# Outer product p7's additions in another order and on GpSimd, the last bias added by pieces, squares summed over both heads of a pair

## The chip, the cores and the metric

The kernel runs on one core of one Trainium2 chip. Its metric is the device time of one execution in microseconds (us). The engines of the core are named as the profile names them: PE is TensorE's matmul side and PEld its weight loads, DVE is VectorE, ACT is ScalarE, POOL is GpSimd, and SP is SyncE, which here only issues DMAs. Each engine runs its own instructions in order, and they wait for each other through semaphores. All numbers are float32.

## The reference

There are 2048 tokens (8 x 256) of 512 values and two layers. The part that the change touches is the first layer's attention, with 32 heads of 128:

```python
qkv = jax.nn.silu(hidden_states @ qkv_w.T)          # 32 heads x (q, k, v) x 128
...
attn = ...                                          # scores with decay, no softmax
xf = xf * jax.lax.rsqrt(jnp.mean(xf * xf, axis=-1, keepdims=True) + EPS)
normed = norm_w * xf.astype(attn.dtype)
gate = jax.nn.sigmoid(hidden_states @ gate_w.T)
return gate * normed @ out_w.T
...
x = x + _L0_attn_ref(xn, ...) + _L0_ffn_ref(xn, ...)
```

The mean of squares runs over all 32 heads (4096 values a token). Beside the attention stands a mixture of 16 experts, two a token, and a shared expert; `sb3` is the bias of the shared expert's last product, 512 values added to every token. A second layer with a small attention and a low-rank mixture follows.

## The kernel before, in words

The tokens are worked in four chunks i = 0 to 3 of 512 (two batches of 256), and the heads in eight groups g of four. A pair (i, g) is a unit. In a unit the projection of a chunk to q, k, gate and v of four heads is done by Strassen's scheme in Winograd's form, on two levels. The outer level has seven products, in the order `p1, p2, p6, p5, p3, p7, p4` (class `Outer`); each of them is itself split in the same way into seven inner products (methods `p1` to `p7` of `Outer`), each written by eight hardware matmuls into a PSUM bank of 128x512. Chunk 0 does four of its seven outer products plainly (`plain`), with eight products, while it builds sums of weights that later chunks load. There are three kinds of banks here: `ps_a` (two), `ps_b` and `ps_e` (one each). For an outer product n the main loop (lines 1318 to 1363) issues its inner p1 and p7, then p3 of outer product n - 1, then p6, p4, p2, p5.

`result` (L1106) reads out each of the four finished quarters (i, j) of an outer product, in the order (1, 0), (0, 0), (1, 1), (0, 1). It puts them together with four accumulators of 128x4x512: `a`, `b`, `c`, `d`. Outer p1 makes `a`, p2 makes `b`, p5 makes `c`, p3 makes `d`; p6, p7 and p4 are first read out from the bank to a temporary `r` (three buffers, tag `sum`, shared with the experts' results `ye` of L820) and then added: p6 and p4 to `a`, p7 to `a` and to `c`. Reading out is a VectorE addition of the bank and an earlier copy (L1134), for the last quarter a ScalarE copy (L1132). The addition to `a` runs on GpSimd (L1135), that to `c`, for p7, on VectorE (L1138). Copies of banks that an inner product goes on accumulating in are made by ScalarE (`copied`, L1101).

When an accumulator is whole, a `Quarter` of attention begins (L1139 to L1141): `b` after p2, `d` after p3, `c` after p7, `a` after p4, for one pair of heads and one batch each. Its pieces (SiLU, gate, scores, attend) are not issued at once. `later(after, f)` (L751) puts a piece into a list with a due slot, and `slot()` (L755), called once after every inner product, issues those that are due: one a slot, two while more than twelve wait; the pieces that its list names (those with little or no work for PE) don't count. There are 49 slots in a unit. The experts' steps, the chunk's ending and the building of tables go the same way. ACT and POOL run their instructions in the order in which the program issues them (L660); on the other engines and for the DMAs the scheduler may move them, except those that are marked to keep their order.

`attend` (L864) squares the 128x512 result of a pair of heads (L884) and adds it on GpSimd to `sums`, 512 values for each batch (L885); the first pair of a chunk is squared into `sums` directly (L881), and after the last pair the two heads' halves are added (L887). `output` (L914) makes sums and differences of gated results `gT` for the output projection, which is Strassen's too; its weights `wo` lie in a ring of seven buffers (L1001). In chunk 1 four differences of these weights are made on GpSimd in every unit (`out_sum`, L1005). The output projection adds up in `acc`, which there is once.

At the end of a chunk, `load_sum` (L1023) reloads the sum `r` of input and shared expert and calls `last_bias` (L651), which loads the bias `sb3` into a buffer of the ring `sum` and issues its four additions to GpSimd at once. After the last projection, `done` (L1030) issues the mean of squares, on POOL the combination of `acc`'s seven parts, on DVE `finish` (L640), which adds the scaled attention to `r`, and a store.

`read_table` (L1204) loads the list of tokens of each expert in two halves, each into the buffer `sq` of the squares; `take_table` copies it out 40 slots later (L1224).

Of the kernel before, what the change touches and what calls it, by code (L numbers as in the profile page):

```python
# [9 lines left out]
FP = mybir.dt.float32  # L10
# [8 lines left out]
B, S, C = 8, 256, 512  # L19
# [51 lines left out]
def block_kernel(  # L71
# [588 lines left out]
    with tc.tile_pool(name="attn", bufs=1) as attn, tc.manual_schedule(engines={mybir.EngineType.Activation, mybir.EngineType.Pool}):  # L660
# [94 lines left out]
        def slot():  # L755

            now[0] += 1
            n = 0
            while pieces and pieces[0][0] <= now[0] and n < (2 if len(pieces) > 12 else 1):
                f = pieces.pop(0)[2]  # L760
                f()
                n += getattr(f, "func", f).__name__ not in ("silu", "bias", "gate", "read_table", "take_table", "scatter", "load_sum", "sums1", "sums2", "sums3", "sums4", "settle0", "settle1", "out_sum", "combine", "finish", "store")


        class Expert:
# [48 lines left out]
            def down(self):  # L814
                py = ps_y()
                mm(  # L816
                    py, self.he, self.we[:, 2 * NC * INTER : 2 * NC * INTER + C],
                    start=True, stop=True,
                )
                ye = attn.tile([P, C], FP, tag="sum", name="ye", bufs=3)  # L820
                add(ye, py, self.xe)
                nc.sync.dma_start(out=yd[bass.ts(self.j, P), :], in_=ye)


        class Quarter:
# [15 lines left out]
            def begin(self):  # L841
                if self.u.g == NG - 1 and (self.pair, self.b) == (1, 0):
                    later(5, self.u.load_sum)
                later(2, partial(self.silu, 0))
                later(3, partial(self.silu, 1))
                later(4, self.gate)
                later(7, partial(self.scores, 0))
                later(8, partial(self.scores, 1))
                later(12, partial(self.attend, 0))
                later(13, partial(self.attend, 1))  # L850
# [13 lines left out]
            def attend(self, hh):  # L864
# [12 lines left out]
                if u.i not in sums_:  # L877
                    sums_[u.i] = attn.tile([P, 2, CH], FP, tag="sums", name="sums")
                sums = sums_[u.i][:, self.b, :]
                if u.g == 0 and self.pair == 0:  # L880
                    nc.scalar.activation(sums, po, AF.Square)  # L881
                else:
                    sq = attn.tile([P, CH], FP, tag="sq" if u.i else "cp", name="sq", bufs=1 if u.i else 5)
                    nc.scalar.activation(sq, po, AF.Square)  # L884
                    add(sums, sums, sq, nc.gpsimd)  # L885
                if u.g == NG - 1 and self.pair == 1:
                    add(sums[:, 0:S], sums[:, 0:S], sums[:, S:], nc.gpsimd)  # L887
                gT = u.gated()
# [11 lines left out]
        class Unit:  # L900
# [122 lines left out]
            def load_sum(self):  # L1023

                if self.i + 1 < NCH:
                    self.r = spare8()
                    nc.sync.dma_start(out=self.r, in_=xr[self.i])
                    last_bias(self.r, attn.tile([P, C], FP, tag="sum", name="sb3", bufs=3))

# [34 lines left out]
        class Outer:  # L1064


            def __init__(self, unit, p):
                self.u, self.p = unit, p
                self.steps = []
                self.following = None  # L1070
# [35 lines left out]
            def result(self, i, j, bank, c):  # L1106
# [22 lines left out]
                else:  # L1129
                    r = attn.tile([P, 512], FP, tag="sum", name="r", bufs=3)  # L1130
                    if c is None:
                        nc.scalar.copy(r, bank)  # L1132
                    else:
                        add(r, bank, c)  # L1134
                    add(a, a, r, pool)  # L1135
                    if p == "p7":
                        c_ = u.tile("c")[:, q]
                        add(c_, c_, r)  # L1138
                whole = dict(p2=("b", 0, 0), p3=("d", 0, 1), p7=("c", 1, 1), p4=("a", 1, 0)).get(p)  # L1139
# [64 lines left out]
        def read_table(n=0):  # L1204
# [18 lines left out]

            later(40, take_table)  # L1224

# [571 lines left out]
```

## Time and profile before

| | |
|---|---|
| time of three runs | 2783.33, 2780.84, 2780.56 us; median 2780.84 |
| the profiled execution | 2780.53 us, of it 2778.5 from the first to the last instruction |
| granted TensorE clock, mean | 0.997 |
| chunk 0 to 3 of the attention | about 130 to 2465 us |
| additions `c<-c,r` on VectorE | 96, 1557 ns mean, 146.7 us |
| additions `c<-c,r` on GpSimd (`a`, from p6, p7, p4) | 264, 1332 ns mean, 345.8 us |
| reading out `r` on VectorE | 240, 684 to 686 ns |

In the profile all of the accumulators are named `c`, and every addition has the line of the helper that records it, L100, so they are told apart by engine and operands. A row of the waits says who waited for whom, how long in total, how often, and at most. A row of the order in time has start, length, engine, line, operation, operands, count, and in brackets how long the engine was idle before it and what ended that. Matmul ends are modelled, and idle times under 0.15 us are taken for the pipeline's own.

### The profile page before, as it was taken

To read this page: it belongs to the slowest core of one execution; us is meant where nothing else is said; L and a number is where in the kernel's file an instruction comes from. 1 tells how busy PE (TensorE), PEld (TensorE's weight loads), DVE (VectorE), ACT (ScalarE), POOL (GpSimd) and SP (SyncE) were. 2 spreads that over 40 slices of the span, in tenths; PEclk is the share of its full clock that TensorE was granted. 3 is DMA by queue.
4 is the path that set the end of the run, shared out by engine and by line. 5 is a ranking of instruction groups with operands and counts; after the bars stand their busy time and mean duration, and the time that the engine had idled before them with its cause. 6 is when DMAs were issued, how large, how long until landed. Compare 5 with 4: busy or idle time off the path is not lost.

```text
span 2778.5 us, 49222 instructions
## 1 busy us (share of the span) xinstructions
PE 2733.5 (98%) x19492; PEld 2522.7 (91%) x19492; DVE 1627.6 (59%) x2733; ACT 947.2 (34%) x1683; POOL 1649.8 (59%) x1422
## 2 busy tenths in 40 slices
PE   9999999999999999999999999999999999999999
PEld 5699999999999999999999999999999999987877
DVE  7656777776545555555545555555555555667663
ACT  5232222222433333333343333334433333432221
POOL 6477777776566666665855555556555567553210
PEclk9999999999999999999999999999999999999999
DMA  7898898888977777777877777787877788653211
GB/s 296 310 339 335 311 334 325 337 315 330 352 274 261 288 272 277 265 280 288 304 250 253 253 257 251 264 288 268 281 255 255 270 298 295 218 215 124 78 63 63
DMA packets 155445, 735.87 MB, mean 265 GB/s; under 512 B 18768, under 2 KB 25296, under 8 KB 112848
## 3 DMA queue, kind: packets, MB, share of 16 engines
q1 hardware_dynamic: 137056, 661.89, 64.8%
q0 software_dynamic: 17872, 70.32, 7.7%
q8 instruction: 154, 2.52, 0.4%
q14 instruction: 75, 0.61, 0.1%
q10 hardware_dynamic: 288, 0.52, 0.1%
HBM read 587.84 MB, written 144.04 MB: 263 GB/s over the span
## 4 chain that ended last, share of the span: by engine, by line
PE 86%; DVE 6%; POOL 3%; issue 3%; DMA 2%; ACT 0%; SPq 0%; DVEq 0%; POOLq 0%; ACTq 0%
PE ps_a L735 25%; PE ps_e L735 13%; PE ps_sc L948 10%; PE ps_b L735 7%; PE ps_sc L968 4%; PE ps_o L869 4%; PE ps_sc L857 3%; PE ps_sc L804 3%; PE ps_o L870 2%; PE ps_sc L858 2%; PE ps_a L1676 2%; PE ps_sc L816 1%; DVE w L100 1%; PE ps_a L1579 1%; PE ps_a L359 1%
## 5 line engine op out<-in xcount | busy, mean ns | idle before, releaser
L735 PE MATMUL ps_a<-xt,w 128*128 128x128 f32 x5376 | 751.3, 276 | 16.3 <-DVE r L100 7.6
L735 PEld LDWEIGHTS ps_a<-xt,w 128*128 128x128 f32 x5376 | 686.7, 192 | 46.0 <-issue 14.1
L100 POOL TENSOR_TENSOR c<-c 128x512 f32<-128x512 f32 x240 | 305.2, 1286 | 265.7 <-DVE c L100 263.1
L1103 ACT COPY cp<-ps_a 128x512 f32<-128x512 f32 x384 | 224.0, 584 | 659.9 <-PE ps_a L735 636.9
L100 POOL TENSOR_TENSOR c<-c,r 128x512 f32<-128x512 f32 x264 | 345.8, 1332 | 167.1 <-DVE r L100 166.6
L735 PE MATMUL ps_e<-xt,w 128*128 128x128 f32 x2688 | 374.5, 275 | 0.6 <-DVE r L100 0.3
L735 PEld LDWEIGHTS ps_e<-xt,w 128*128 128x128 f32 x2688 | 341.4, 192 | 6.7 <-issue 2.9
L735 PE MATMUL ps_a<-w,xt 128*128 128x128 f32 x1792 | 346.8, 275 | 0.0
L100 POOL TENSOR_TENSOR w<-w 128x512 f32<-128x512 f32 x224 | 297.7, 1337 | 80.5 <-DVE w L100 32.9
L100 POOL TENSOR_TENSOR sums<-sums,sq 128x512 f32<-128x512 f32 x120 | 155.8, 1298 | 277.4 <-ACT sq L884 276.8
L948 PE MATMUL ps_sc<-wo,gT 128*128 128x256 f32 x1288 | 304.9, 380 | 2.8 <-POOL gT L100 2.8
L735 PEld LDWEIGHTS ps_a<-w,xt 128*128 128x128 f32 x1792 | 272.4, 192 | 0.0
L948 PEld LDWEIGHTS ps_sc<-wo,gT 128*128 128x128 f32 x1288 | 232.9, 190 | 30.9 <-POOL gT L100 3.1
L100 DVE TENSOR_TENSOR acc<-ps_sc,acc 128x512 f32<-128x512 f32 x208 | 142.7, 689 | 195.2 <-PE ps_sc L948 150.6
L891 DVE SCALAR_TENSOR_TENSOR gT<-ps_o,nw,c 128x256 f32<-128x256 f32 x256 | 112.0, 479 | 216.1 <-ACT sq L884 206.0
L735 PE MATMUL ps_b<-xt,w 128*128 128x128 f32 x1536 | 214.8, 276 | 6.5 <-issue 3.7
L100 DVE TENSOR_TENSOR c<-ps_a,c 128x512 f32<-128x512 f32 x216 | 146.8, 687 | 120.7 <-PE ps_a L735 115.4
L735 PEld LDWEIGHTS ps_b<-xt,w 128*128 128x128 f32 x1536 | 195.1, 193 | 9.0 <-issue 5.7
L832 ACT ACTIVATE c<-c 128x512 f32<-128x512 f32 x256 | 150.3, 628 | 146.0 <-DVE c L100 127.9
L884 ACT ACTIVATE sq<-ps_o 128x512 f32<-128x512 f32 x120 | 71.7, 597 | 358.1 <-PE ps_o L870 352.7
L100 DVE TENSOR_TENSOR s<-ps_sc,decay 128x384 f32<-128x384 f32 x256 | 139.7, 553 | 79.9 <-PE ps_sc L858 77.2
L735 PE MATMUL ps_e<-w,xt 128*128 128x128 f32 x896 | 173.5, 275 | 0.0
(297 smaller groups left out, 4723.3 us busy)
## 6 DMA issues: line engine op xcount, KB each, us to landing
w<-in_w_att_dram SPq DMA_DIRECT2D x56, 1024.0 KB
w<-in_w_att_dram SPq DMA_DIRECT2D x72, 768.0 KB
st<-in_w_att_dram SPq DMA_DIRECT2D x32, 1024.0 KB
wo<-in_w_out_dram SPq DMA_DIRECT2D x113, 256.0 KB
decay<-dec SPq DMA_DIRECT2D x64, 384.0 KB
w<-ws0p SPq DMA_DIRECT2D x12, 1792.0 KB
w<-ws1p SPq DMA_DIRECT2D x12, 1792.0 KB
w<-ws2p SPq DMA_DIRECT2D x12, 1792.0 KB
```

Of the source, the lines that this page charges most:

```text
L100: (eng or nc.vector).tensor_tensor(o, a, b, op)
L735: mm(bank[:, bass.ts(ty, P)], a, b, start=(first and ty == 0), stop=True, skip_group_check=True,)
L804: mm(pu[:, bass.ts(n, P)], w12[:, n, c, :], self.xeT[:, c, :], start=(c == 0), stop=(c == NC - 1),)
L832: nc.scalar.activation(qk, qk, AF.Silu)
L857: mm(p[:, 0:S], self.c[:, 2 * hh, P : 2 * P], q, start=True, stop=True)
L858: mm(p[:, S : S + P], self.c[:, 2 * hh + 1, P : 2 * P], q[:, 1, :], start=True, stop=True,)
L869: mm(po[:, bass.ts(hh, S)], v[:, 0, :], self.s[:, hh, 0:S], start=True, stop=False)
L884: nc.scalar.activation(sq, po, AF.Square)
L891: nc.vector.scalar_tensor_tensor(gT[:, h, :].rearrange("p (t n) -> p t n", t=2), po[:, bass.ts(h, S)].rearrange("p (t n) -> p t n", t=2), ...
L948: mm(py[:, bass.ts(t, S)], self.O[p][:, hh, bass.ts(t, P)], self.wo[p][:, hh, :], start=(t == 0 and hh == 0), stop=(hh == 1), skip_group_c ...
L968: mm(py[:, bass.ts(h, S)], gT[:, hh, bass.ts(t, P)], self.wo[pair, h][:, hh, :], start=(h == 0 and hh == 0), stop=(hh == 1), skip_group_ch ...
L1103: nc.scalar.copy(c, bank)
```

## The change

- In `result`, for p7 outside chunk 0, the additions to `c` go to GpSimd at each readout, and those to `a` to VectorE. The latter are collected and issued after the third readout (three of them), and after the fourth.
- `r` and `ye` have four buffers. The room comes from `sums`, which holds 256 values for each batch instead of 512: each square goes to a buffer of its own, and its two heads' halves are added to `sums` by two instructions (one for the first pair).
- `load_sum` is issued after one slot instead of five. The bias goes to a buffer of the ring `wo`, and its four additions become pieces 10, 13, 16 and 19 slots later, which don't count in a slot.
- `take_table` comes after 30 slots.

```diff
@@ slot
-                n += getattr(f, "func", f).__name__ not in ("silu", "bias", "gate", ...
+                n += getattr(f, "func", f).__name__ not in ("bias_sum", "silu", "bias", "gate", ...
@@ Expert.down
-                ye = attn.tile([P, C], FP, tag="sum", name="ye", bufs=3)
+                ye = attn.tile([P, C], FP, tag="sum", name="ye", bufs=4)
@@ Quarter.begin
-                    later(5, self.u.load_sum)
+                    later(1, self.u.load_sum)
@@ Quarter.attend
-                    sums_[u.i] = attn.tile([P, 2, CH], FP, tag="sums", name="sums")
+                    sums_[u.i] = attn.tile([P, 2, S], FP, tag="sums", name="sums")
                 sums = sums_[u.i][:, self.b, :]
+                sq = attn.tile([P, CH], FP, tag="sq" if u.i else "cp", name="sq", bufs=1 if u.i else 5)
+                nc.scalar.activation(sq, po, AF.Square)
                 if u.g == 0 and self.pair == 0:
-                    nc.scalar.activation(sums, po, AF.Square)
+                    add(sums, sq[:, 0:S], sq[:, S:], nc.gpsimd)
                 else:
-                    sq = attn.tile([P, CH], FP, tag="sq" if u.i else "cp", name="sq", bufs=1 if u.i else 5)
-                    nc.scalar.activation(sq, po, AF.Square)
-                    add(sums, sums, sq, nc.gpsimd)
-                if u.g == NG - 1 and self.pair == 1:
-                    add(sums[:, 0:S], sums[:, 0:S], sums[:, S:], nc.gpsimd)
+                    for h in range(2):
+                        add(sums, sums, sq[:, bass.ts(h, S)], nc.gpsimd)
@@ Unit.load_sum
-                    last_bias(self.r, attn.tile([P, C], FP, tag="sum", name="sb3", bufs=3))
+                    b3_t = attn.tile([P, C], FP, tag="wo", name="sb3", bufs=7)
+                    nc.sync.dma_start(out=b3_t, in_=b3[E : E + 1].to_broadcast([P, C]))
+
+                    def bias_sum(t):
+                        add(self.r[:, t, :], self.r[:, t, :], b3_t, nc.gpsimd)
+
+                    for t in range(TPC):
+                        later(10 + 3 * t, partial(bias_sum, t))
@@ Outer
-                self.steps = []
+                self.steps, self.added = [], []
...
-                    r = attn.tile([P, 512], FP, tag="sum", name="r", bufs=3)
+                    r = attn.tile([P, 512], FP, tag="sum", name="r", bufs=4)
                     if c is None:
                         nc.scalar.copy(r, bank)
                     else:
                         add(r, bank, c)
-                    add(a, a, r, pool)
-                    if p == "p7":
+                    if p != "p7":
+                        add(a, a, r, pool)
+                    else:
                         c_ = u.tile("c")[:, q]
-                        add(c_, c_, r)
+                        add(c_, c_, r, pool)
+
+                        self.added.append(partial(add, a, a, r))
+                        if (i, j) in ((1, 1), (0, 1)):
+                            while self.added:
+                                self.added.pop(0)()
@@ read_table
-            later(40, take_table)
+            later(30, take_table)
```

More of the change, by code (lines that the diff above doesn't have):

```diff
@@ L761, in slot @@
                 f()
-                n += getattr(f, "func", f).__name__ not in ("silu", "bias", "gate", "read_table", "take_table", "scatter", "load_sum", "sums1", "sums2", "sums3", "sums4", "settle0", "settle1", "out_sum", "combine", "finish", "store")
+                n += getattr(f, "func", f).__name__ not in ("bias_sum", "silu", "bias", "gate", "read_table", "take_table", "scatter", "load_sum", "sums1", "sums2", "sums3", "sums4", "settle0", "settle1", "out_sum", "combine", "finish", "store")
         class Expert:
```

## The prediction

> **What bounds the kernel now.** I read the page's first part, then the chain of waits, then TensorE's own list of waits, and last the instructions in order of time around each wait.
>
> ```profile
> PE 2733.5 (98%) x19492; PEld 2522.7 (91%) x19492; DVE 1627.6 (59%) x2733; ACT 947.2 (34%) x1683; POOL 1649.8 (59%) x1422
> PE 86%; DVE 6%; POOL 3%; issue 3%; DMA 2%; ACT 0%; SPq 0%; DVEq 0%; POOLq 0%; ACTq 0%
> ```
>
> TensorE is busy for 2733.5 of 2778.5 us and holds 86% of the chain. The change touches no matmul, so it can win only out of the 45 us in which TensorE idles, and it loses only where it makes TensorE wait. The list of TensorE's waits (us in total, times, longest) names the part within reach:
>
> ```profile
> PE ps_a L735 <- DVE r L100: 7.6, 16, 1.3
> PE ps_a L735 <- ACT cp L1103: 5.2, 3, 1.8
> ...
> PE ps_sc L948 <- POOL gT L100: 2.8, 2, 1.6
> ```
>
> Asked by stretches, the sixteen waits for `r` all lie in chunks i = 1 to 3: thirteen of 0.4 us, two of 0.5, one of 1.3. Chunk 0 has none. Here is one of the thirteen, in order of time (start, length, instruction; idle before it in brackets):
>
> ```profile
> 1445.35 0.69 DVE L100 TENSOR_TENSOR r<-ps_e,cp 128x512 f32<-128x512 f32 x1 [1.19 <-PE ps_e L735]
> 1446.12 1.27 POOL L100 TENSOR_TENSOR c<-c,r 128x512 f32<-128x512 f32 x1 [4.09 <-DVE r L100]
> 1446.14 1.80 DVE L100 TENSOR_TENSOR c<-c,r 128x512 f32<-128x512 f32 x1
> 1446.84 0.83 PE L735 MATMUL ps_a<-xt,w 128*128 128x128 f32 x6
> 1447.73 0.83 PE L735 MATMUL ps_e<-xt,w 128*128 128x128 f32 x6
> 1447.87 0.68 DVE L100 TENSOR_TENSOR r<-ps_b,cp 128x512 f32<-128x512 f32 x1
> 1448.47 0.68 DVE L100 TENSOR_TENSOR r<-ps_a,cp 128x512 f32<-128x512 f32 x1
> 1448.62 4.62 POOL L100 TENSOR_TENSOR c<-c,r 128x512 f32<-128x512 f32 x3 [1.23 <-DVE r L100]
> 1449.06 4.73 DVE L100 TENSOR_TENSOR c<-c,r 128x512 f32<-128x512 f32 x3
> 1449.20 0.94 PE L735 MATMUL ps_a<-xt,w 128*128 128x128 f32 x6 [0.41 <-DVE r L100]
> ```
>
> Products start 0.89 us apart (1446.84, 1447.73), so the next was due at 1448.63. It came at 1449.20, 0.57 late, because it accumulates into the bank that the third `r` reads out. That readout stood behind an addition of 1.80 us on VectorE.
>
> **The change, part by part.**
>
> *Outer product p7 (96 additions to `c` leave VectorE for GpSimd, 96 to `a` go the other way).* Counts stay, order changes: the readouts come first, and VectorE's additions follow in a burst after the third. In the stretch above the second readout can begin about 0.13 us after its bank is done, near 1446.25, and the third near 1447.15, ending 1447.85. The product is due at 1448.63: slack 0.8, the whole 0.57 is won. Thirteen such places: **-7.4 us**.
>
> What is late next? Single additions on VectorE take 0.68 us with GpSimd still, 1.75 to 1.80 beside a GpSimd addition, and GpSimd's own take 1.27, or 1.73 when one of VectorE's gets between. The Trainium skill ("SBUF — State Buffer", section "SBUF: two separate sides") has a rule that speaks against the swap: a VectorE operation with two SBUF inputs and a GpSimd operation that reads SBUF exclude each other for the whole instruction, so moving additions between the two frees nothing. By the rule, eight additions hold the port for 4 x 0.68 + 4 x 1.27 = 7.8 us either way; the trace has 1446.12 to 1453.80, 7.7 us, and agrees. I take no gain of engine time, and the gain above is order alone. It differs on one price: under the rule a VectorE addition caught by GpSimd lasts 1.27 + 0.68 = 1.95, the row says 1.80 at most, and four at the rule's price would end 0.6 us later. I take the row.
>
> So VectorE's fourth addition ends near 1453.8 as before, while TensorE is 0.57 ahead. The following Outer's third readout ended at 1456.53 for a product at 1457.52: slack 0.99 becomes 0.42. Nothing is given back.
>
> `c` feeds the next quarter of attention, and its last addition is now GpSimd's fourth instead of VectorE's. In the trace GpSimd's fourth (to `a`) already ends 0.58 us or more before that SiLU starts in fifteen of the sixteen units of chunks 2 and 3 (the last unit I leave out), so ScalarE starts no later there. In chunk 1, GpSimd's queue holds the four output-weight differences and an expert's bias gather between the third and fourth addition:
>
> ```profile
> 1149.72 1.29 POOL L100 TENSOR_TENSOR wo<-wo 128x512 f32<-128x512 f32 x1
> 1150.12 1.14 ACT L832 ACTIVATE c<-c 128x512 f32<-128x512 f32 x2
> 1150.95 2.51 POOL L100 TENSOR_TENSOR c<-c,r 128x512 f32<-128x512 f32 x2
> 1156.30 0.83 PE L735 MATMUL ps_a<-xt,w 128*128 128x128 f32 x6
> ```
>
> There the fourth ends at 1152.23, 2.1 us after the SiLU starts. The SiLU waits; queued behind it on ScalarE are two SiLUs, gate and tanh, then the bank copy that started 2.84 us after it. That copy would end at 1152.27 + 2.84 + 0.56 = 1155.67, and its product starts at 1156.30: slack 0.63, cost 0 in seven units. In unit (1,0) the delay is 3.7 us and eats part of what is won there.
>
> *Four buffers for `r` instead of three.* Two waits of 0.65 us (1380.8 and 1969.2, units (2,0) and (3,0)) and the one of 1.49 (772.1) are readouts that wait for a buffer held by GpSimd's backlog. A fourth buffer removes both of the first, -1.2, and about 0.9 of the third, after 0.5 given back to the late SiLU: **-2.1 us**. Experts' results share this ring; three `r` held for the burst leave one.
>
> *Last bias.* Now GpSimd stands before four additions until a transfer lands:
>
> ```profile
> 1309.78 0.33 SPq L653 DMA_DIRECT2D sb<-in_b_dram  x1
> 1322.60 4.96 POOL L100 TENSOR_TENSOR spare<-spare,sb 128x512 f32<-128x512 f32 x4 [11.43 <-DMA sb<-in_b_dram]
> ```
>
> It waits 11.4 us, adds for 5.0, and the gated differences behind it hold TensorE for 1.8 us at 1328.9 (the list's 1.6 and its ramp). The other two places (721 and 1901) hold up nothing on TensorE. Afterwards the two DMAs issue four slots earlier on SyncE, the additions come one by one from ten slots on, some 15 us after the issue (a unit of 49 slots takes 73 to 76 us) against 12.7 us to landing. **-1.8 us.** The bias takes a buffer of the output weights' ring; each following weight load then reuses the next tile along, released two slots or more before: nothing. The slots of all other pieces stay within two of their place; the `finish` steps keep theirs, so the two 1.8 us waits for ScalarE's copies (1364, 1952), which stand behind `finish`, stay.
>
> *Squares.*
>
> ```profile
> L100 POOL TENSOR_TENSOR sums<-sums,sq 128x512 f32<-128x512 f32 x120 | 155.8, 1298 | 277.4 <-ACT sq L884 276.8
> L100 POOL TENSOR_TENSOR sums<-sums 128x256 f32<-128x256 f32 x8 | 5.8, 726 | 0.6
> ```
>
> 120 additions of 1.298 become 240 of 0.726, eight of 0.726 move from the end to the beginning: GpSimd +18.4 us, 0.15 each quarter, at 59% load. ScalarE's 128 squares stay. Cover: GpSimd's idle time. It is thin in chunk 0, where TensorE waits five times, 3.2 us, for weight sums on GpSimd: five delays of 0.15 would be 0.8, none falling there 0. I take +0.5. The wait for `gT` at 2334 grows by 0.15.
>
> *Table read ten slots earlier.* It frees the `sq` buffer for chunk 1's first square, which now uses it. Its VectorE copy runs 30 slots, some 45 us, after the read's issue: nothing.
>
> Sum: -7.4 - 2.1 - 1.8 + 0.65 = -10.7 us. Each removed wait lets later work arrive sooner, and waits under 0.15 us are not listed; I keep nine tenths, -9.5. Against the profiled execution (2778.5 us span, 2780.53 in all) that is 2771.0; the median shown, 2780.84, is 0.3 us above it. **Forecast 2771 us**, 0.35% faster. Own range: 2768 (all 12.5 won without cost) to 2775 (half).
>
> **Rivals.**
>
> *The wait returns one Outer later.* The slack of 0.42 in front of the following Outer's product is used up, as VectorE's burst ends half a microsecond late. For it: additions of 1.8 us exist. Against: the port's sum is unchanged. Then the thirteen win nothing, and 2.1 + 1.8 - 0.65 remain: about 2777, no change that can be measured (0.2%, 5.6 us, is what this kernel's times tell from none).
>
> *The burst holds VectorE: slower.* If all four additions run at 1.8, they end at 1447.85 + 7.2 = 1455.05, 1.25 later than now. In thirteen units of chunks 2 and 3 the next readout is then 1.25 - 0.42 = 0.83 late against 0.57 won: +3.4. In chunk 1 the burst stands in front of the expert's transposed rows (a copy that ends at 1147.72 for a product at 1147.86): 1.1 late in seven units, +7.7. With -3.3 elsewhere: +7.8, about 2788. It decides from a mean of 1.6 us for these additions (now 1.557). Against it: a burst begun while GpSimd works catches the same gaps between its additions as today.
>
> *The new order isn't what the engines run.* VectorE's order is not held by hand except for marked steps; if the additions to `a` are put between the readouts again, only buffers and bias pay: 2777, as the first rival.
>
> **Chances.** Forecast 0.66; the wait returns or the order is not kept, 0.18; slower 0.16. Single ends shift a little: faster by over 0.2% 0.66, within 0.17, slower 0.17. A range of 2767 to 2782 holds the forecast's cases and nearly all of the middle.
>
> **What would show it.** TensorE's list loses the sixteen waits for `r`, and the one for `gT` near 1329; the additions to `a` on VectorE stand three in a row after the third readout; GpSimd's `spare` additions stand singly with no idle time for `sb`; GpSimd is 18 us busier. It is wrong if waits for ScalarE's `cp` appear in chunk 1 (late SiLU), for `xeT` (burst), or for weights in chunk 0.

## The result, and the profile after

The changed kernel takes 2775.07 us (median of 20 runs, 2770.12 to 2782.01), the kernel before beside it on the same chip 2782.01 us (20 runs). The ratio is **0.9975, 95% interval 0.9968 to 0.9982**: 0.25% faster, or some 7.0 us (5.0 to 8.9) of 2780.84. The forecast was 0.35%, 9.5 us. The profiled execution took 2772.59 us with a span of 2770.6, against 2780.53 and 2778.5.

The first part of the page (busy us, share of the span, instructions):

```profile
PE 2730.1 (99%) x19492; PEld 2523.7 (91%) x19492; DVE 1614.9 (58%) x2733; ACT 949.2 (34%) x1683; POOL 1682.5 (61%) x1542
```

TensorE's instructions are as many as before, and GpSimd has 120 more and is 33 us busier: 25 from the squares (187.0 for 161.6; forecast 18, at 0.726 us each; they took 0.75) and 14 from slower additions to the accumulators, less what other groups lost. TensorE's list of waits (us in total, times, longest):

```profile
PE ps_a L735 <- ACT cp L1109: 6.5, 3, 2.3
PE ps_a L735 <- POOL w L100: 3.9, 5, 1.4
...
PE ps_e L735 <- DVE r L100: 2.1, 3, 1.0
...
PE ps_sc L947 <- POOL gT L100: 1.4, 1, 1.4
```

The row of sixteen waits of `ps_a` for `r`, 7.6 us, is gone, and so is one of the two for `gT`. Four rows of the attention have grown: ScalarE's copies from 5.2 to 6.5, weight sums from 3.2 to 3.9, `ps_e` waiting for `r` from 0.3 to 2.1, and `ps_o` waiting for `s` (chunk 0) from 1.3 to 1.8.

The list counts from the modelled end of the matmul before, which lies 0.16 us behind the start that its successor has without a wait; so each wait is 0.16 us longer than listed (0.57 where the row in the prediction has 0.41; the prediction calls this a ramp). So I also took, for each matmul, the time from its start to the next one's, less the median for its kind, and added up what exceeds 0.12 us:

| TensorE's lost time, us | before | after |
|---|---|---|
| before chunk 0, to 130 us | 9.7 | 9.6 |
| chunk 0, 130 to 755 us | 15.5 | 16.5 |
| chunks 1 to 3, 755 to 2470 us | 17.6 | 10.4 |
| after 2470 us | 10.3 | 9.7 |

In chunks 1 to 3 the thirteen waits of 0.57 are gone (7.4), that of 1.49 at 772 and that of 1.81 at 1329. Against them stand +1.3 at two chunk endings (1.83 and 1.84 became 2.50 and 2.48), +1.0 in units (2,0) and (3,0) (0.65 twice became 1.18 and 1.10), and 1.4 in four small places.

The table still leaves out that the next matmul after a late one follows it by 0.21 us instead of 0.11. The time from one unit's first readout of p7 to the next unit's has this in it: from unit (2,1) on it was 73.18 us before (1445.35 to 1518.53) and is 72.50 now (1444.87 to 1517.37). In nine units nothing else changed, and they are 0.67 to 0.70 us shorter. So my estimate for the thirteen waits is 13 x 0.68 = 8.8 us; the new waits have the same addition, and the sum for chunks 1 to 3 stays near the 7.2 of the table.

Here is the place that the prediction showed, unit (2,1), in the changed kernel, in order of time:

```profile
1444.87 0.69 DVE L100 TENSOR_TENSOR r<-ps_e,cp 128x512 f32<-128x512 f32 x1 [1.19 <-PE ps_e L735]
1445.66 0.69 DVE L100 TENSOR_TENSOR c<-c,r 128x512 f32<-128x512 f32 x1
1445.70 6.38 POOL L100 TENSOR_TENSOR c<-c,r 128x512 f32<-128x512 f32 x4 [4.22 <-DVE r L100]
1446.27 0.69 DVE L100 TENSOR_TENSOR r<-ps_b,cp 128x512 f32<-128x512 f32 x1
1446.87 0.68 DVE L100 TENSOR_TENSOR r<-ps_a,cp 128x512 f32<-128x512 f32 x1
...
1447.47 5.16 DVE L100 TENSOR_TENSOR c<-c,r 128x512 f32<-128x512 f32 x3
...
1448.14 0.83 PE L735 MATMUL ps_a<-xt,w 128*128 128x128 f32 x6
```

The product at 1448.14 has no wait. But **the order on VectorE is not the forecast one**: readout, addition, readout, readout, three additions is the kernel before's own order. The additions were collected in the program, and the scheduler, which may move VectorE's unmarked instructions, put the first behind the first readout again. What differs is its length: 0.69 us where it was 1.80. And it now begins at 1445.66, 0.04 ahead of GpSimd's at 1445.70; before, GpSimd's began at 1446.12 and VectorE's at 1446.14.

Measured from the end of the first readout, this is so in every one of twenty p7 of chunks 1 to 3 (the other four of the 24 have another order or other starts there):

| | GpSimd's addition begins | VectorE's addition begins | VectorE's takes | GpSimd's takes |
|---|---|---|---|---|
| before | 79 ns | 104 ns | 1.80 us | 1.27 us |
| after | 143 to 144 ns | 104 ns | 0.69 us | 1.79 us |

Thirteen of the twenty, those of chunks 2 and 3, had the waits of 0.57. The seven of chunk 1 had the same 1.80 before and lost 0.14 at most: there an expert's four matmuls (L786, 0.44 us) stand ahead of the product that needs the bank.

The groups say the same over all additions (busy us, mean ns):

```profile
L100 POOL TENSOR_TENSOR c<-c,r 128x512 f32<-128x512 f32 x264 | 359.4, 1384 | 154.1 <-DVE r L100 153.5
...
L100 DVE TENSOR_TENSOR c<-c,r 128x512 f32<-128x512 f32 x96 | 135.3, 1438 | 2.1
```

VectorE's fell from 1557 to 1438 ns, GpSimd's rose from 1332 to 1384. In all the additions take 494.7 us against 492.5: nothing was saved, only the one that waits changed.

### The profile page after: what moved, and what is told of

It is laid out like the page before. It is cut to its first block, busy times and chain, and to the rows that moved or that the text cites. A ratio compares the mean times of both kernels' runs of the same rounds, so it can differ in the third digit from the quotient of the medians.

```text
span 2770.6 us, 49302 instructions
## 1 busy us (share of the span) xinstructions
PE 2730.1 (99%) x19492; PEld 2523.7 (91%) x19492; DVE 1614.9 (58%) x2733; ACT 949.2 (34%) x1683; POOL 1682.5 (61%) x1542
## 5 line engine op out<-in xcount | busy, mean ns | idle before, releaser
L735 PE MATMUL ps_a<-xt,w 128*128 128x128 f32 x5376 | 751.0, 276 | 10.7 <-ACT cp L1109 6.5
L100 POOL TENSOR_TENSOR c<-c,r 128x512 f32<-128x512 f32 x264 | 359.4, 1384 | 154.1 <-DVE r L100 153.5
L100 POOL TENSOR_TENSOR sums<-sums,sq 128x256 f32<-128x256 f32 x240 | 180.2, 751 | 287.1 <-ACT sq L881 277.3
L100 DVE TENSOR_TENSOR acc<-ps_sc,acc 128x512 f32<-128x512 f32 x208 | 142.7, 689 | 203.3 <-PE ps_sc L947 161.6
```

The lines of the kernel that those rows point to most:

```text
L100: (eng or nc.vector).tensor_tensor(o, a, b, op)
L735: mm(bank[:, bass.ts(ty, P)], a, b, start=(first and ty == 0), stop=True, skip_group_check=True,)
```

## The experiments

**Theory 1:** the 7.4 us come from who begins first after the first readout (before, GpSimd by 25 ns; after, VectorE by 40). The one that comes second waits for the other. If that is VectorE, the second and third readouts stand behind it and TensorE waits; if it is GpSimd, nobody does. **Theory 2** (the prediction's): they come from taking the additions from between the readouts. **Theory 3:** they come from which engine adds to which accumulator, whoever begins first. The recorded expectations count their theories anew for each run: their "theory 2" is theory 2 here for the first four kernels, theory 3 for dve_later2 and dve_later3, and the prediction's slower rival for forced.

### Who begins first: six kernels

*at_once*: the changed kernel, additions to `a` issued at each readout.

```diff
-                        self.added.append(partial(add, a, a, r))
-                        if (i, j) in ((1, 1), (0, 1)):
-                            while self.added:
-                                self.added.pop(0)()
+                        add(a, a, r)
```

> The changed kernel, but VectorE's additions to a are issued at each readout, not collected behind the third. Theory 1 (the thirteen 0.57 us waits vanished because VectorE's first addition is first at the port, 0.69 us instead of 1.80; collecting changed nothing in VectorE's order): no wait of TensorE for r on ps_a in chunks 2 and 3, the first addition of a group at about 0.69, span within 2 us of 2770.6. Theory 2 (collecting keeps the readouts free): the thirteen waits of 0.4 us return, span about 2778.

*collect_only*: the changed kernel, `a` on GpSimd and `c` on VectorE as before, still collected.

```diff
-                        add(c_, c_, r, pool)
+                        add(a, a, r, pool)
...
-                        self.added.append(partial(add, a, a, r))
+                        self.added.append(partial(add, c_, c_, r))
```

> The changed kernel, but a stays with GpSimd and c with VectorE as before; VectorE's additions (to c) are still collected. Theory 1: GpSimd's addition to a waits for one engine only, starts before VectorE's, the first addition of a group takes 1.80 and the thirteen waits of 0.4 us stay (0.57 each, 7.4 us): span 2776 to 2779. Theory 2 (order alone): the waits are gone, span about 2771.

*pool_later*: the kernel before, and one tiny copy on GpSimd.

```diff
+                    if p == "p7" and (i, j) == (1, 0):
+                        pool.tensor_copy(small.tile([P, 1], FP, tag="tiny", name="tiny"), r[:, 0:1])
                     add(a, a, r, pool)
```

> The kernel before with one instruction more in each p7: GpSimd copies one column of the first r to a spare tile ahead of its first addition to a, so that this addition starts some 0.1 us later. Nothing else is changed. Theory 1: VectorE's first addition is first at the port and takes about 0.7 us; the thirteen waits vanish, span 2770 to 2772 with everything else as before. Theory 2: nothing changes, span 2778 to 2779.

*dve_later*: the changed kernel, and one tiny copy on VectorE. The condition around it is the same as in pool_later.

```diff
+                        if (i, j) == (1, 0):
+                            tiny = small.tile([P, 1], FP, tag="tiny", name="tiny")
+                            self.added.append(partial(nc.vector.tensor_copy, tiny, r[:, 0:1]))
                         self.added.append(partial(add, a, a, r))
```

> The changed kernel with a copy of one column of the first r on VectorE ahead of its first addition to a, which so starts 0.06 to 0.2 us later. Theory 1: GpSimd's addition comes first, VectorE's takes 1.7 to 1.8 us, and thirteen waits of 0.4 us or more return: span about 2778. Theory 2: span 2771 as in the changed kernel.

*dve_later2*: three such copies, each reading the one before.

```diff
+                            for n in range(3):
+                                self.added.append(partial(nc.vector.tensor_copy, tiny[:, n : n + 1], tiny[:, n - 1 : n] if n else r[:, 0:1]))
```

> The changed kernel, and VectorE copies one column of the first r, and then that column twice more, one after the other, before its first addition to a (in all chunks but the first). The earlier trial with one such copy still began the addition 104 ns after the readout, so nothing had been delayed. Theory 1 (the gain is who begins first after the first readout): three dependent copies push VectorE's addition beyond GpSimd's 144 ns; GpSimd's addition to c then begins first, VectorE's takes about 1.8 us instead of 0.69, the second readout is late, and the thirteen waits of about 0.4 us for r are back: about 7 us slower than the changed kernel, near 2779 to 2781. Theory 2 (the gain is which engine adds to which accumulator): the roles are as in the changed kernel, so no wait comes back and the time stays within 1.5 us of it, near 2772. If the first addition still begins before 144 ns, both expect about 2772 and nothing is told apart.

*dve_later3*: the three copies again, with readouts, copies and additions held in program order, and the first addition issued right behind the first readout.

```diff
-                        add(r, bank, c)
+                        ins = nc.vector.tensor_tensor(r, bank, c, ALU.add)
+                        if p == "p7":
+                            tc.keep_in_program_order(ins)
...
+                        if (i, j) == (1, 0):
+                            tiny = small.tile([P, 3], FP, tag="tiny", name="tiny")
+                            for n in range(3):
+                                kept(nc.vector.tensor_copy(tiny[:, n : n + 1], tiny[:, n - 1 : n] if n else r[:, 0:1]))
-                        self.added.append(partial(add, a, a, r))
-                        if (i, j) in ((1, 1), (0, 1)):
+                        self.added.append(lambda a=a, r=r: kept(nc.vector.tensor_tensor(a, a, r, ALU.add)))
+                        if (i, j) != (0, 0):
```

> The changed kernel with the same three dependent copies of one column of the first r ahead of VectorE's first addition to a, and VectorE's copies, readouts and additions of p7 held in program order: readout, three copies, addition, readout, readout, two additions. In the trial before this one the scheduler had put two of the three copies behind the third readout, so that the addition still began at 104 ns. Theory 1 (who begins first after the first readout): the three copies take about 70 ns each, VectorE's addition begins some 200 to 300 ns after the readout, GpSimd's addition to c at 144 ns comes first, VectorE's takes about 1.8 us instead of 0.68, and thirteen waits for r are back, each 0.57 us or up to 0.2 more: near 2780, at or above the kernel before less 1 us. Theory 2 (which engine adds to which accumulator): no waits come back, 2772 to 2773.

Measured (ratio to the kernel before, with its interval; begins are after the first readout's end):

| | ratio | GpSimd begins | VectorE's addition begins, takes | waits of 0.57 |
|---|---|---|---|---|
| at_once | 0.9964 (0.9950 to 0.9977) | 144 ns | 104 ns, 0.69 us | none |
| collect_only | 1.0001 (0.9992 to 1.0010) | 79 ns | 104 ns, 1.80 us | thirteen |
| pool_later | 0.9974 (0.9964 to 0.9984) | 67 ns the copy, 217 ns the addition | 104 ns, 0.69 us | none |
| dve_later | 0.9968 (0.9956 to 0.9980) | 144 ns | 104 ns, 0.68 us | none |
| dve_later2 | 0.9975 (0.9965 to 0.9986) | 143 ns | 105 ns, 0.68 us | none |
| dve_later3 | 1.0007 (0.9998 to 1.0016) | 144 ns | 481 ns, 1.48 us | twelve, 0.61 to 0.99 |

**Theory 2 falls**, as the account of what this change won, with the first two: without collecting the whole gain is there, and without the exchange there is none, though collect_only keeps the collecting and the rest of the change (bias, buffers and squares, which nearly cancel, see below). It is no test of a true burst: the scheduler put its first addition between the readouts too, at 104 ns. That test is forced, below. **Theory 3 falls** with pool_later and dve_later3. pool_later is the kernel before with nothing changed but a copy of one column, 182 ns, in front of GpSimd's addition. Here is its place in unit (2,1), VectorE's rows and then GpSimd's, in order of time:

```profile
1447.85 0.69 DVE L100 TENSOR_TENSOR r<-ps_e,cp 128x512 f32<-128x512 f32 x1 [1.19 <-PE ps_e L735]
1448.64 0.69 DVE L100 TENSOR_TENSOR c<-c,r 128x512 f32<-128x512 f32 x1
1449.25 0.68 DVE L100 TENSOR_TENSOR r<-ps_b,cp 128x512 f32<-128x512 f32 x1
...
1448.60 0.18 POOL L1136 COPY tiny<-r 128x1 f32<-128x1 f32 x1 [4.07 <-DVE r L100]
1448.75 4.63 POOL L100 TENSOR_TENSOR c<-c,r 128x512 f32<-128x512 f32 x3
```

VectorE's addition is the first of the two now, takes 0.69, and the second readout follows at once. By the ratio it gains as much as the whole change, 7.2 us, though in its profile the wait for `gT` at 1327 grew to 3.1 us.

dve_later and dve_later2 missed and tell nothing against a theory, since nothing was delayed. One copy fits into the 104 ns in which the addition waits for `r` anyway (readout ends 1446.86, copy 1446.89, addition 1446.96):

```profile
1446.89 0.15 DVE L1153 COPY tiny<-r 128x1 f32<-128x1 f32 x1
1446.96 0.68 DVE L100 TENSOR_TENSOR c<-c,r 128x512 f32<-128x512 f32 x1
```

Of three, the scheduler put two behind the third readout. Held in order they delay the addition, and the changed kernel loses its gain though each engine adds to the accumulator it had. The rows of VectorE, then GpSimd, in dve_later3:

```profile
1448.56 0.69 DVE L1140 TENSOR_TENSOR r<-ps_e,cp 128x512 f32<-128x512 f32 x1 [1.19 <-PE ps_e L735]
1449.28 0.15 DVE L1153 COPY tiny<-r 128x1 f32<-128x1 f32 x1
1449.47 0.34 DVE L1153 COPY tiny<-tiny 128x1 f32<-128x1 f32 x2
1449.73 1.49 DVE L1154 TENSOR_TENSOR c<-c,r 128x512 f32<-128x512 f32 x1
1451.14 0.68 DVE L1140 TENSOR_TENSOR r<-ps_b,cp 128x512 f32<-128x512 f32 x1
...
1449.39 1.28 POOL L100 TENSOR_TENSOR c<-c,r 128x512 f32<-128x512 f32 x1 [4.22 <-DVE r L1140]
```

GpSimd comes first (1449.39 against 1449.73) and takes its own 1.28; VectorE's addition takes 1.49, and the second readout begins at 1451.14, though its bank was done at 1449.3. Twelve of the waits are back; the thirteenth, of unit (3,6), did not come:

```profile
PE ps_a L735 <- DVE r L1140: 6.0, 12, 0.8
```

The delay by the copies would not have been enough: they set the addition back by 0.38 us, and in the changed kernel the third readout ends at 1447.55 and the product begins at 1448.14, 0.59 later, where 0.05 is enough when TensorE waits. So 0.53 us were to spare. The other 0.80 us come from being second (1.49 for 0.69). Together that is 0.38 + 0.80 - 0.53 = 0.65 too late, and eleven of the twelve waits cost 0.61 to 0.65.

**Theory 1 is shown in both directions**, for a GpSimd that stands idle before its addition. For one that is at work before it, the starts in the rows do not tell who wins (unit (2,0), below).

Why GpSimd's addition begins later in the changed kernel can be read from the waits in the traces. The first addition to `c` needs two semaphores, VectorE's and GpSimd's own (GpSimd had written `c`), and GpSimd has a wait instruction of its own for VectorE's in front of it; that to `a` needs VectorE's only and waits for it itself. In the kernel before I took all of GpSimd's additions to accumulators that VectorE released after over 0.4 us of idle time. The 80 that wait for VectorE themselves begin 78 to 87 ns after its end, the 69 with the wait instruction in front 134 to 152 ns, and none lies between. In the changed kernel there are 68 and 58 with the same bounds. No run varied this wait by itself.

### The forecast's own order

*forced*: VectorE's readouts of p7 and its additions held in program order, so that three additions really stand behind the third readout.

```diff
-                        add(r, bank, c)
+                        ins = nc.vector.tensor_tensor(r, bank, c, ALU.add)
+                        if p == "p7":
+                            tc.keep_in_program_order(ins)
...
-                        self.added.append(partial(add, a, a, r))
+                        self.added.append(lambda a=a, r=r: tc.keep_in_program_order(nc.vector.tensor_tensor(a, a, r, ALU.add)))
```

> The changed kernel, with VectorE's readouts of p7 and its additions to a held in the order in which the program issues them, so that the three additions really stand behind the third readout, as the prediction had it. Theory 1 (in the changed kernel the gain is the 25 ns of the race): with no VectorE addition between the readouts there is no race, so no wait of 0.57 comes back and TensorE has the same 7.4 us less idle time as in the changed kernel; the additions, issued later and beside GpSimd's, are slow (1.2 to 1.8 us each), and the fourth ends up to 1.3 us later than now. Near 2771 to 2773. Theory 2 (the prediction's slower rival: the burst holds VectorE): waits for xeT in chunk 1 and for the next Outer's r appear, 5 us or more of them, and the time is near 2778 or above.

Ratio 0.9976 (0.9966 to 0.9987), as the changed kernel: the burst loses the thirteen waits too. VectorE's additions average 1379 ns (1557 before). The slower rival came in kind, but small: in seven units of chunk 1 the product that reads `xeT` is 0.21 us late, of which 0.05 is idle time, so that the list of waits doesn't have it. That is 1.5 us in all, where the rival had 1.1 in each, and the next Outer's `r` brings no new wait. It also loses the waits of units (2,0) and (3,0). Here is what differs. VectorE in the changed kernel, unit (2,0), and then GpSimd:

```profile
1369.16 0.68 DVE L100 TENSOR_TENSOR r<-ps_a,cp 128x512 f32<-128x512 f32 x1
1369.76 6.47 DVE L100 TENSOR_TENSOR c<-c,r 128x512 f32<-128x512 f32 x2
1376.16 0.68 DVE L100 TENSOR_TENSOR ye<-ps_sc,xw 128x512 f32<-128x512 f32 x1
...
1379.04 0.69 DVE L100 TENSOR_TENSOR r<-ps_e,cp 128x512 f32<-128x512 f32 x1 [0.67 <-DMA yd<-ye]
...
1369.03 1.07 POOL L777 DMA_INDIRECT xw<-in_w_exp_dram,rows__1101  x1 [0.30 <-issue]
1370.13 4.95 POOL L100 TENSOR_TENSOR c<-c,r 128x512 f32<-128x512 f32 x4
```

and in forced:

```profile
1369.36 0.69 DVE L1140 TENSOR_TENSOR r<-ps_a,cp 128x512 f32<-128x512 f32 x1
1369.97 1.93 DVE L1149 TENSOR_TENSOR c<-c,r 128x512 f32<-128x512 f32 x3
1373.81 0.69 DVE L100 TENSOR_TENSOR ye<-ps_sc,xw 128x512 f32<-128x512 f32 x1 [1.91 <-DMA xw<-in_b_dram,own__1102]
...
1377.91 0.69 DVE L1140 TENSOR_TENSOR r<-ps_e,cp 128x512 f32<-128x512 f32 x1 [0.21 <-DMA yd<-ye]
```

GpSimd comes to p7 late there, with four additions ready to run without a gap. In the changed kernel the first of the two VectorE additions takes 5.87 us of the 6.47. It begins at 1369.76, while GpSimd is at an indirect DMA (1369.03 to 1370.10), and ends at 1375.63, 0.55 us after the last of GpSimd's four. (The loser in unit (2,1) before ended 0.55 us after GpSimd's addition as well: 1447.94 and 1447.39.) The expert's result `ye` stands behind it and leaves late, and the next readout waits until the store of `ye` frees its buffer in the ring. In forced the three additions are over (1371.9) before GpSimd begins (1372.2).

By the rows VectorE began first here, by 0.37 us, and yet it waited for all four. The indirect DMA by itself is not what held it: twelve of VectorE's additions in the kept traces lie wholly within such a DMA and took 0.68 to 0.72 us. One of them, in bias_only, GpSimd's DMA and additions with it:

```profile
1958.95 1.00 POOL L777 DMA_INDIRECT xw<-in_w_exp_dram,rows__1101  x1 [0.30 <-issue]
1959.08 0.69 DVE L100 TENSOR_TENSOR c<-c,r 128x512 f32<-128x512 f32 x1
1959.96 4.95 POOL L100 TENSOR_TENSOR c<-c,r 128x512 f32<-128x512 f32 x4
```

Slow (5.6 to 5.9 us) were the five that still ran when GpSimd's addition followed the DMA after 15 to 27 ns; they had begun 0.11 to 0.38 us ahead of it, in four kernels. Against them stand 145 places over all traces where GpSimd was idle, or at the tiny copy, before its addition: there a VectorE addition that began up to 0.64 us ahead by the rows was never slow. Why the five lost is open.

### The other terms

*bias_only*: the kernel before with the bias's part of the change alone (ring `wo`, four pieces, issued after one slot; the lines are those of the diff above).

```diff
-                    later(5, self.u.load_sum)
+                    later(1, self.u.load_sum)
...
-                    last_bias(self.r, attn.tile([P, C], FP, tag="sum", name="sb3", bufs=3))
+                    b3_t = attn.tile([P, C], FP, tag="wo", name="sb3", bufs=7)
```

> The kernel before with the last bias alone changed: loaded after one slot into the ring of the output weights, added in four pieces. Both theories of p7 expect the thirteen waits of 0.57 to stay. The prediction's term for the bias, 1.8 us, expects the wait for gT at 1329 to go and nothing to come instead: 2776.5 to 2777.5 of span near 2776.7. A rival: GpSimd's four pieces, now among the chunk's ending, delay its sums elsewhere, and less than 1 us is left.

Ratio 0.9993 (0.9984 to 1.0001): 1.9 us, though the interval reaches no change. The wait at 1329 is gone and that at 772 fell from 1.49 to 0.56; the thirteen stay. The fall at 772 can't be put down to the bias alone: in pool_later, which has the old bias and the old buffers, this wait is 0.58 too.

*squares_bufs*: the kernel before with the squares, the four buffers and the table's 30 slots; p7 and bias as before.

```diff
+                sq = attn.tile([P, CH], FP, tag="sq" if u.i else "cp", name="sq", bufs=1 if u.i else 5)
+                nc.scalar.activation(sq, po, AF.Square)
                 if u.g == 0 and self.pair == 0:
-                    nc.scalar.activation(sums, po, AF.Square)
+                    add(sums, sq[:, 0:S], sq[:, S:], nc.gpsimd)
...
-                    r = attn.tile([P, 512], FP, tag="sum", name="r", bufs=3)
+                    r = attn.tile([P, 512], FP, tag="sum", name="r", bufs=4)
```

> The kernel before with the squares by halves, four buffers for r and ye, and the table taken ten slots earlier; p7 and the bias as before. Both theories of p7 expect the thirteen waits of 0.57 to stay. The prediction's terms: -2.1 for the buffers (waits at 772, 1381 and 1969 for r gone or shorter), +0.65 for the squares: about 1.5 us faster. The other reading, from the trace of the changed kernel: there the waits near 1381 and 1969 grew to 1.1 us each, the two waits for ScalarE's copies behind finish grew from 1.8 to 2.5, and chunk 0's waits for weight sums by 0.9 in all. If the squares and the fourth buffer are what did this, this kernel shows it too: cp waits of 6 us or more in the list, weight sums 3.9, and a time within 1 us of before or above it. If it is the p7 swap, the cp waits stay at 5.2 and the waits near 1381 and 1969 are gone.

Ratio 1.0008 (1.0002 to 1.0015), 2.2 us slower. The fourth buffer does what it was forecast to do: the waits at 1381 and 1969 are gone (0.26 is left near the first), and so is the one at 772. The kernel is slower all the same. The two waits behind `finish` are 2.49 each, as in the changed kernel, and chunk 0 lost 17.5 us (a wait of 1.4 at 130 us is counted to the stretch before). That last is uncertain: over all profiles chunk 0 lost 15.5 to 16.2 in the three kernels with the old squares and 15.2 to 17.9 in those with the new, about 1 more in the mean, and the profiles differ by 2 us before 130 us too, where the programs are alike. These places don't add up to the measured time: chunks 1 to 3 lost 17.1 us (17.6 before), and with 1 us for chunk 0 the kernel would be 0.5 us slower. The rest of the 2.2 (0.6 to 4.2) is not located.

The cause of the longer waits at the endings is in GpSimd's queue. Its rows, and then VectorE's `finish` (L646), in squares_bufs:

```profile
1356.22 1.27 POOL L100 TENSOR_TENSOR acc<-acc 128x512 f32<-128x512 f32 x1
1357.44 0.73 POOL L100 TENSOR_TENSOR sums<-sq 128x256 f32<-128x256 f32 x1
1358.13 2.96 POOL L100 TENSOR_TENSOR acc<-acc 128x512 f32<-128x512 f32 x2
1361.05 4.61 POOL L100 TENSOR_TENSOR c<-c 128x512 f32<-128x512 f32 x3
...
1361.46 4.75 DVE L646 SCALAR_TENSOR_TENSOR spare<-acc,rms,spare 128x512 f32<-128x512 f32 x3
```

The chunk's first `sums<-sq` is new here; the square was made by ScalarE alone before. It pushes the three additions to `c` back, and they then cover the three `finish` steps, which take 4.75 us; in the kernel before they began 1.1 us ahead of them (1359.50, 1360.60) and the steps took 4.09. *first_on_vector* takes this one addition away from GpSimd.

```diff
-                    add(sums, sq[:, 0:S], sq[:, S:], nc.gpsimd)
+                    add(sums, sq[:, 0:S], sq[:, S:], nc.gpsimd if u.i == 0 else nc.vector)
```

> The changed kernel, with the first square of a chunk (chunks 1 to 3) put together on VectorE instead of GpSimd: one addition of 128x256 that stood in GpSimd's queue ahead of the last step of acc's combination and of three additions to c. Theory: this one addition, new in the change, pushed those three additions under the last finish steps and so made the two waits for ScalarE's copies longer; without it they are back at 1.8 us each instead of 2.5 (the chunk endings near 1361 and 1947), some 1.3 us faster than the changed kernel, near 2770 to 2771. Rival: the growth comes from the fourth buffer or from another place of the three additions; then both waits stay at 2.5 or change by less than 0.2, and the time is that of the changed kernel within 1 us.

Both waits fell from 2.5 to 2.0, three quarters of the growth and between the two expectations' figures; `finish` takes 4.26. That addition is most of the cause, and not all of it. (The waits of units (2,0) and (3,0) are shorter here as well, 0.81 and 0.37 for 1.18 and 1.10.) Ratio 0.9964 (0.9953 to 0.9976).

### A better version

*ending_early*: the changed kernel with the combination of `acc` and `finish` two slots earlier; *forced_early*: the same on top of forced.

```diff
-                after = 2
+                after = 0 if 0 < i < NCH - 1 else 2
```

> The changed kernel, with GpSimd's combination of acc and the finish steps of chunks 1 and 2 two slots earlier. In the changed kernel the last three finish steps on VectorE run beside three additions to c on GpSimd, take 4.76 us and hold ScalarE's copy into acc and, queued behind it, two bank copies: TensorE waits 2.50 and 2.48 us. My theory: two slots are about 3 us, the steps then stand in front of those additions and both waits go: -4 to -5 us, near 2767 to 2768. Rival: GpSimd is full there (its additions follow one another without a gap), so the combination ends hardly earlier, finish still waits for it, and VectorE, held in its order by the waiting finish, reads out banks late: no gain, or up to 2 us slower.

> Both at once: the changed kernel with VectorE's p7 readouts and additions held in program order (the true burst, which lost the waits of 1.1 us near 1381 and 1969 as well), and the chunk's ending two slots earlier. If both gains stand, the stretch from 755 to 2465 us, which holds 10.3 us of TensorE's idle time in the changed kernel and 9.1 with the burst alone, is down to 4 to 5: near 2766. If the earlier ending gains nothing: near 2772, as with the burst alone.

ending_early: 0.9958 (0.9944 to 0.9972). The long waits became 0.70 each, but a new one of 0.54 and 0.57 stands just before, as the rival had it in part: two steps of `finish`, begun with no idle time behind GpSimd's combination, take 1.78 and 1.75 us beside GpSimd's additions and hold a readout behind them on VectorE. So 5.0 us became 2.5. forced_early: **0.9950 (0.9937 to 0.9964), 2768.23 us**, faster than both kernels; chunks 1 to 3 lose 7.1 us, from 10.4 (expected were 4 to 5). The row of its list that was 6.5 in the changed kernel:

```profile
PE ps_a L735 <- ACT cp L1109: 2.9, 3, 1.8
```

## Why the prediction was right, and where it was wrong

**Direction and bound: right.** TensorE's instructions did not change, and of the 7.9 us between the two profiled spans 6.9 are in the table of its lost time. (The lower end of its range counts "all 12.5 won"; the waits that the prediction lists add up to 7.4 + 1.3 + 1.5 + 1.8 = 12.0.)

**The p7 term, -7.4: right in size, wrong in its reason.** The step that failed is "the readouts come first, and VectorE's additions follow in a burst after the third". The scheduler kept the old order, which the prediction had as its third rival. But that rival's number, 2777, failed as well: with the old order collect_only wins nothing, and the changed kernel wins all thirteen waits, because the exchange of roles turned the race at the first addition. The start times stood in the prediction's own rows, 1446.12 for GpSimd and 1446.14 for VectorE; I read the 1.80 as the price of a VectorE addition there, and not as the price of being second. That the term held is luck: the order that it was worked out for never ran. The order itself would have been worth it, as forced shows. (By the length of the units the term was rather 8.8.)

**The rule weighed: right, and read by half.** "SBUF — State Buffer", section "SBUF: two separate sides", says that the one which starts first has the shared pair for its whole instruction. I took from it that the sum of the lock times can't change, and the sum did not (494.7 against 492.5 us). Its other half, who starts first, was the whole gain of p7. It holds by the rows at 145 places and not at five, where GpSimd came straight from a DMA. On the price, the row was nearer: the loser took 1.80 or 1.79, not the 1.95 I had made of the rule for a VectorE addition caught from the start.

**The late SiLU, cost 0: held.** It starts later in chunk 1, and no wait for a copy follows it there: from 755 to 1340 us TensorE lost 0.7 us in all. **The wait returning one Outer later did not come. The slower rival's wait for `xeT` came in the true burst only**, with 0.21 us instead of 1.1 in each of seven units.

**The buffers, -2.1: right alone for the two waits of 0.65, undone here.** Both vanish in squares_bufs. In the changed kernel they became 1.18 and 1.10, since the exchange set a VectorE addition against GpSimd's four in a row, and `ye` behind it holds a buffer. With the wait at 772, -1.5 and +1.0 make -0.5.

**The bias, -1.8: right**, 1.81 at 1329. "The two 1.8 us waits for ScalarE's copies, which stand behind `finish`, stay" was wrong: +1.3, mostly by the square's addition that moved "from the end to the beginning". I had priced its 0.73 us as engine time, and not looked at what it stands in front of. **Squares, +0.65:** chunk 0 lost some 1.0 more, of uncertain size; with the endings they cost about 2.3.

By these terms the -10.7 becomes -7.4 - 0.5 - 1.8 + 2.3 = -7.4, and the small new waits in chunks 1 to 3, `gT` at 2327 among them, bring it to -6.0. The profiles show -6.2 for chunks 0 to 3, and another -0.7 where the change touches nothing. Measured over all runs were 7.0.

## What to carry to other kernels

When two engines take up work on the same result at almost the same moment and exclude each other, look at which begins first, to the nanosecond: the length of the loser's row is the price of its place, and what stands behind the loser pays it. Let the engine with the urgent queue begin first, by its dependencies or by an order that is held, and don't count on a program's order that the scheduler may move. An operation moved to another time is priced by what it now stands in front of, not by its own length.

## What the runs showed of the hardware that was not expected

- A difference of 25 ns in the start decides over 1.1 us of an instruction and, at thirteen places, over 7 us of the kernel. The starts are steady to a nanosecond or two: 78 to 80, 103 to 106 and 143 to 145 ns after the readout, at the twenty places where GpSimd stands idle.
- The 65 ns between GpSimd's two starts go with a separate wait instruction in front of the addition: 78 to 87 ns without it, 134 to 152 with it, in all 149 cases of the kernel before.
- A VectorE addition took 5.87 us beside four GpSimd additions without a gap: it did not get in between them, though it had begun 0.37 us before the first. GpSimd was at an indirect DMA when it began; twelve additions that lie wholly within such a DMA took 0.68 to 0.72, so the DMA alone is not the cause, which is open.
- VectorE's addition begins 104 ns after the end of the readout that it depends on, and a copy of one column set between them cost nothing (104 to 106 ns in dve_later).
